# Layer 0 of a sequence model on one core: VectorE's token work with one PSUM operand, in halves inside the groups, and beta added to x ahead of time

## The chip, the cores and the metric

One kernel runs on one core of a Trainium2 chip. TensorE (PE) multiplies matrices and writes its results to PSUM; VectorE (DVE), ScalarE (ACT) and GpSimd (POOL) work elementwise; SyncE (SP) issues most of the DMAs. Each engine takes its own instructions in the order in which the program issues them, and waits for the others through semaphores. The metric is the device time of one execution in microseconds (us); lower is better.

## The reference, cut to what matters

```python
x = x + L0(_layernorm(x))        # a recurrence over 512 tokens, 8 sequences, width 128
x = x + FFN(_layernorm(x))       # six layers: local attention (16 heads, window 32) and a gated FFN

def L0(x):                       # x here is the normalised input
    xb = einsum('bsd,ed->sbe', x, B)
    h, y = tanh(h @ A.T + xb_t), h @ C.T          # token after token
    out = ys + x
    mu, var = mean(out), mean((out - mu) ** 2)
    return (out - mu) * rsqrt(var + 1e-5) * gamma + beta
```

So a token of the six layers is made in this way: y from the recurrence, plus the normalised input, a layernorm with gamma and beta ("the first norm"), plus x, and a second layernorm ("the second norm"). The first of those sums, x1, is also needed at the very end, and goes to DRAM. The tokens then enter the attention of the first layer of six; "layer 0" below is that first layer, which starts while the recurrence still runs.

## The kernel before, in words

**Chunks.** The 512 tokens are four chunks of 128; a chunk is a tile of 128 tokens on the partitions by 8 sequences by 128 features. `Recurrence.first(c)` loads x of a chunk (xc), normalises it (xn, pieces `a` and `b`), writes xn to DRAM, and turns it (piece `d`). It runs for chunk 0 at the start, and for chunks 1 to 3 between the first steps of the recurrence.

**Steps.** `step` is one token of the recurrence: a matmul of A with the last state into a PSUM bank that already holds B times the input (the tile xb), and a tanh on ScalarE. Inside the attention work a step is slipped in by `tick`, after each batch of matmuls. Where there is no other work, `alone` issues a step and two more matmuls that nobody reads (tile warm).

**Tokens of a chunk.** After the last step of a chunk, `queue(c)` makes a list of pieces: `output` (C times the states, in two halves of four sequences, tile yp, added to o), the first norm of o (`stats`, `rsqrt`, `normalise`), `scale` (times gamma, plus beta), `add` (x1 = x + o, to DRAM), the second norm of x1 into o, and `turn` for each half of the sequences (four transposes into PSUM, tile rt_c, and two ScalarE copies into xT, the token tile of the attention). All pieces between `output` and `turn` are VectorE's and work from SBUF to SBUF. `rsqrt` is eleven small instructions on 128 x 8 numbers.

**Groups.** The attention of layer 0 goes by groups: (chunk c, half h of the sequences, head group g), in the order of `parts`. A group is four slots, t = 0 to 3; each slot of `mixed` (used for the first nine groups, NREC) holds stages of several groups at once: scores (tile sc), max and exp, transposes (tp, at), the average (av), and for the group after next four "units" in slots 2 and 3. A unit is `unit_a` and `unit_b`: two matmuls (rawa, rawb), ScalarE squares, a VectorE product and two GpSimd operations of 128 x 1024. In slot 0 VectorE solves reciprocal roots (`Norms.solve`); in slot 1 these are spread by matmuls (tile bc) and multiplied in by `finish`, which also issues the DMAs to qT and kbuf; then four matmuls of `project` (tile yo). Later groups and layers use `dense`.

**What sets the order.** Program order, written out by hand: `run(k)` inside `mixed` puts the stages of `fill[k]` and then one waiting piece of the token work; in slot 1 only at k = 0, or pieces that need no PSUM bank. `begin(n)` calls `rec.need(c)` before the first group of a chunk: there all pieces that are left are issued at once, and if the recurrence has not got that far, steps alone.

**PSUM.** The pool "mm" has three banks while the recurrence runs. yp, rt_c, warm, raw, bc, yo and the others take turns in it.

Of the kernel before, what the change touches and what calls it, by code (L numbers as in the profile page):

```python
# [7 lines left out]
F32 = mybir.dt.float32  # L8
# [40 lines left out]
def mk_seq_preln_kernel(  # L49
# [28 lines left out]
    )  # L78
    x1_d = dram.tile([P, NT, B, D], F32, name="x1_d")
    xn_d = dram.tile([P, NT, B, D], F32, name="xn_d")  # L80
    xnT_d = dram.tile([P, NT, P, B], F32, name="xnT_d")
    kh_d = dram.tile([4, P, GP, NT, WINDOW], F32, name="kh_d")
    vh_d = dram.tile([4, 2, QB, NT, GP, VW], F32, name="vh_d")
# [68 lines left out]
    with tc.tile_pool(name="qk", bufs=2) as qkp, tc.tile_pool(  # L152
# [16 lines left out]
        class Recurrence:  # L169
# [17 lines left out]
                return x[:, c * P : (c + 1) * P, :].rearrange("b p d -> p b d")  # L187

            def stats(self, src, nm, bs=range(B)):
                if bs[0] == 0:  # L190
                    self.mv = small.tile([P, B, 2], F32, tag="mv", name=f"mv_{nm}", bufs=1)
                mv = self.mv
                for b in bs:
                    st = small.tile([P, 6], F32, tag="st", name=f"st_{nm}_{b}", bufs=4)
                    nc.vector.bn_stats(st, src[:, b, :])
                    nc.vector.bn_aggr(mv[:, b, :], st)

            def rsqrt(self, nm):
                x_, y, a = (
                    small.tile([P, B], F32, tag=f"r{i}", name=f"{i}_{nm}", bufs=1)  # L200
                    for i in "xya"
                )
                nc.vector.tensor_scalar_add(x_, self.mv[:, :, 1], EPS)
                nc.vector.tensor_scalar(
                    y.bitcast(I32), x_.bitcast(I32), -0.5, RSQRT_SEED, ALU.mult, ALU.add
                )
                for _ in range(3):
                    nc.vector.scalar_tensor_tensor(a, x_, -0.5, y, ALU.mult, ALU.mult)
                    nc.vector.tensor_mul(a, a, y)
                    nc.vector.scalar_tensor_tensor(y, a, 1.5, y, ALU.add, ALU.mult)  # L210
                self.rs = y

            def normalise(self, dst, src, bs=range(B)):
                for b in bs:
                    nc.vector.tensor_scalar(
                        dst[:, b, :],
                        src[:, b, :],
                        self.mv[:, b, 0:1],
                        self.rs[:, b : b + 1],
                        ALU.subtract,  # L220
                        ALU.mult,
                    )

            def turned(self, src, nm, q):

# [7 lines left out]
            def first(self, c):  # L233

                nm = f"a{c}"
                xc = self.load(c, self.x_of(c), "xc", "t", 4)
                xn = tmp.tile([P, B, D], F32, tag="sq", name=f"xn_{c}", bufs=4)
                if c:
                    xnT = tmp.tile([P, P, B], F32, tag="u", name=f"xnT_{c}")
                else:  # L240
                    xnT = self.xnT[0] = recp.tile([P, P, B], F32, tag="xnT", name="xnT_0")

                def a():
                    self.stats(xc, nm)

                def b():
                    self.rsqrt(nm)
                    self.normalise(xn, xc)
                    nc.sync.dma_start(xn_d[:, c], xn)

                def d():
                    for q in range(B // 4):
                        nc.vector.tensor_copy(
                            xnT[:, :, 4 * q : 4 * q + 4].rearrange("p t b -> p b t"),
                            self.turned(xn, nm, q),
                        )
                    if c:
                        nc.sync.dma_start(xnT_d[:, c], xnT)

                return [a, b, d]  # L260

            def step(self):
                t = self.t
# [25 lines left out]
                nc.scalar.activation(self.hT[:, tl, :], self.xb[:, k, :], AF.Tanh)  # L289
                self.t, self.work = t + 1, 0.0  # L290
                if tl == P - TB // 2:
                    self.o = self.load(c, xn_d[:, c], "o", "xf", 2)
                    self.x1 = self.load(c, self.x_of(c), "x1", "xf", 2)
                if tl == P - 1:
                    self.queue(c)
                    self.held = True
# [18 lines left out]
            def queue(self, c):  # L315
                o, x1 = self.o, self.x1

                def scale(bs):
                    g, b = (
                        gb[:, i : i + 1, :].to_broadcast([P, B // 2, D]) for i in range(2)  # L320
                    )
                    nc.vector.tensor_mul(o[:, bs, :], o[:, bs, :], g)
                    nc.vector.tensor_add(o[:, bs, :], o[:, bs, :], b)

                def add():
                    nc.vector.tensor_add(x1, x1, o)
                    nc.sync.dma_start(x1_d[:, c], x1)

                def turn(q):
                    tp = self.turned(o, f"c{c}", q)  # L330
                    sq = slice(4 * q, 4 * q + 4)
                    nc.scalar.copy(xT[:, sq, c * P : (c + 1) * P], tp)
                    nc.scalar.copy(self.edge[D // 2 :, sq, c], tp[D // 2 :, :, P - 1])
                    if q:
                        self.posted = c + 1

                def norm(dst, src, nm):
                    for b in range(0, B, 2):
                        yield lambda b=b: self.stats(src, nm, (b, b + 1)), False
                    yield lambda: self.rsqrt(nm), False  # L340
                    for b in range(0, B, 4):
                        yield lambda b=b: self.normalise(dst, src, range(b, b + 4)), False


                self.pieces = [(lambda q=q: self.output(c, o, q), True) for q in range(2)]
                self.pieces += norm(o, o, f"b{c}")
                self.pieces += [(lambda: scale(slice(0, 4)), False)]
                self.pieces += [(lambda: scale(slice(4, 8)), False), (add, False)]
                self.pieces += norm(o, x1, f"c{c}")
                self.pieces += [(lambda q=q: turn(q), True) for q in range(2)]  # L350

            def piece(self, bank=True):
                if self.pieces and (bank or not self.pieces[0][1]):
# [20 lines left out]
                if self.t < S and self.work >= PACE and not self.held and not late:  # L374
                    self.step()

            def need(self, c):

                while self.posted <= c:
                    if self.pieces:  # L380
                        self.piece()
                    else:
                        self.alone()

        rec = Recurrence()

# [551 lines left out]
        def begin(n):  # L938
# [3 lines left out]
            if l == 0:  # L942
                c, h = b
                if g == 0:
                    rec.need(c)
                    xs = shifted_chunk(c, h, buf)
                groups[n] = ChunkGroup(n, c, h, g, xs)
                return
# [10 lines left out]
        def mixed(n, t, cur, one, two, old, last, lt, back, bt):  # L959
# [21 lines left out]
            def run(k):  # L981
                for f in fill[k]:
                    f()
                if t != 1 or k == 0:
                    rec.piece()
                elif k < 4:
                    rec.piece(False)

            run(0)
            if cur:  # L990
# [3 lines left out]
            if back:  # L994
                back.turn_back(bt)
            run(1)
            if cur:
                cur.less_max(t)
            run(2)
# [5 lines left out]
                one.mask(0)  # L1005
            if one and t == 1:
                one.finish(1)
            if last:
                last.average(lt)
            if one and t == 1:  # L1010
                one.finish(2)
# [118 lines left out]
        with tc.manual_schedule():  # L1130
# [12 lines left out]
            while rec.t < P:  # L1143
                if rec.t % 8 == 7 and ahead:
                    ahead.pop(0)()
                rec.alone()
            for _ in range(2):
                rec.piece()
            while rec.posted == 0:
                rec.piece()  # L1150
                rec.alone()
            for t in (2, 3):
                slot(-2, t)
            feed = soon = None
            for n in range(-1, len(todo) + 1):
                m, l = n % GL, n // GL
                if n == NREC:
                    rec.need(NT - 1)
                    recs.close()
                    mmp = mms.enter_context(tc.tile_pool(name="mm", bufs=4, space=PSUM))  # L1160
                    ffn_w = load_ffn_weights(0)
# [142 lines left out]
```

## Time and profile before

| what | us |
|---|---|
| median of three runs | 3785.76 (3784.16 to 3793.64) |
| the profiled execution | 3782.38 |
| its span, first to last instruction | 3780.7 |
| PE busy, share of the span | 3549.9, 94% |
| VectorE busy | 2589.3, 68% |
| GpSimd busy | 1824.6, 48% |
| granted TensorE clock, mean of the span | 0.976 |

The recurrence takes place in the first 598 us of the span; what the change touches of the attention lies before 660 us. In the windows of the profile, the stretch from 0 to 650 us has granted clocks from 0.76 to 1.00, the stretch after it mostly 1.00. A busy share is read with care: PE's matmuls are pipelined and their ends are modelled, and an engine can be busy with an operation that itself is held up.

A group without token work lasts about 44 us while the recurrence runs: the scores matmuls of its four slots start at 291.68, 300.87, 316.51 and 324.47, and those of the next group at 335.81.

### The profile page before, as it was taken

The page shows a single profiled execution, that of the slowest core. Times are in us where ns is not written, and L with a number is a line of the kernel's source. Part 1 is how long each engine was busy: PE and PEld are TensorE (multiplying, and loading weights), DVE is VectorE, ACT ScalarE, POOL GpSimd, SP SyncE. Part 2 cuts the span into 40 slices and gives each one's busy share as a digit, 9 for nine tenths or more (in the row PEclk, how much of TensorE's full clock was granted, in tenths as well). Part 3 has the DMA queues.
Part 4 walks back from the last instruction along what each step waited for, and adds up shares of the span by engine and source line. Part 5 has one row for each costly group of instructions (what it writes and reads, how often), then busy time and mean ns, then how long its engine had stood idle before and what let it go on. Part 6 is the DMA issues. An engine that isn't in the chain of part 4 may idle for free.

```text
span 3780.7 us, 159055 instructions
## 1 busy us (share of the span) xinstructions
PE 3549.9 (94%) x70180; PEld 2140.3 (57%) x70180; DVE 2589.3 (68%) x5208; ACT 1932.6 (51%) x3864; POOL 1824.6 (48%) x780
## 2 busy tenths in 40 slices
PE   8889987999999999999999999999999999999997
PEld 4556665545556565556565555565565555555553
DVE  3455555767677677677677677677677677677673
ACT  2344443545555465455455455455455455455552
POOL 1333333625366366366366366365365355365450
PEclk9888988999999999999999999999999999999998
DMA  4233443554355355345356355355355355355342
GB/s 127 58 90 80 102 93 74 126 114 112 86 119 120 75 120 134 85 107 127 70 118 140 76 113 120 71 128 129 80 118 118 77 133 127 80 122 114 78 107 61
DMA packets 366074, 390.51 MB, mean 103 GB/s; under 512 B 96846, under 2 KB 262220, under 8 KB 365260
## 3 DMA queue, kind: packets, MB, share of 16 engines
q1 hardware_dynamic: 364380, 378.09, 43.8%
q8 instruction: 554, 9.08, 1.1%
q10 hardware_dynamic: 1008, 2.27, 0.2%
q14 instruction: 132, 1.08, 0.1%
HBM read 34.56 MB, written 14.20 MB: 13 GB/s over the span
## 4 chain that ended last, share of the span: by engine, by line
PE 75%; DVE 11%; SPq 4%; issue 4%; ACT 3%; DMA 3%; DVEq 0%; ACTq 0%
PE rawa L526 8%; PE rawb L538 8%; PE sc L627 7%; PE yo L713 5%; PE av L674 4%; PE nsq L430 4%; PE tp L656 4%; PE yf L912 3%; PE xb L281 3%; PE fa L886 3%; PE vps L587 3%; PE fg L890 3%; PE at L703 3%; SPq L574 3%; DMA xbuf<-xT 3%
## 5 line engine op out<-in xcount | busy, mean ns | idle before, releaser
L548 POOL TENSOR_TENSOR u<-rope_sb,bs 128x1024 f32<-128x1024 f32 x320 | 764.5, 2389 | 1263.1 <-ACT bs L544 901.5
L549 POOL TENSOR_TENSOR t<-t,u 128x1024 f32<-128x1024 f32 x320 | 757.3, 2367 | 25.1
L516 DVE SCALAR_TENSOR_TENSOR t<-rawa,par_sb,rope_sb 128x1024 f32<-128x1024 f32 x320 | 410.5, 1283 | 237.0 <-ACT sq L530 223.2
L565 DVE TENSOR_TENSOR t<-t,bc 128x1024 f32<-128x1024 f32 x320 | 381.8, 1213 | 13.6 <-PE bc L465 8.2
L650 ACT ACTIVATE e<-e 128x512 f32<-128x512 f32 x320 | 201.8, 630 | 354.4 <-DVE e L643 238.0
L526 PE MATMUL rawa<-xbuf,wqk 128*128 128x512 f32 x640 | 346.5, 623 | 30.5 <-DMA xbuf<-xT 30.3
L661 ACT COPY eT<-tp 128x512 f32<-128x512 f32 x320 | 190.2, 594 | 349.9 <-PE tp L656 349.2
L674 PEld LDWEIGHTS av<-vbuf,eT 64*32 64x32 f32 x20480 | 228.5, 105 | 218.7 <-issue 145.1
L538 PE MATMUL rawb<-xbuf,wqk 128*128 128x512 f32 x640 | 345.0, 621 | 0.0
L587 PE MATMUL vps<-wv,xbuf 128*64 128x256 f32 x2560 | 316.7, 386 | 7.8 <-DVE xf L864 6.6
L713 PE MATMUL yo<-aoT,wo 128*128 128x512 f32 x640 | 318.8, 621 | 0.9 <-ACT aoT L707 0.9
L627 PEld LDWEIGHTS sc<-kbuf,qT 64*32 64x32 f32 x20480 | 227.1, 105 | 146.5 <-issue 49.9
L674 PE MATMUL av<-vbuf,eT 64*32 64x65 f32 x20480 | 286.9, 225 | 6.7 <-issue 5.3
L640 DVE TENSOR_REDUCE mx<-sc 128x8 f32<-128x512 f32 x320 | 219.4, 686 | 103.7 <-PE sc L627 103.7
L692 DVE TENSOR_TENSOR ao<-av,rc 128x256 f32<-128x256 f32 x640 | 271.6, 424 | 22.0
L627 PE MATMUL sc<-kbuf,qT 64*32 64x64 f32 x20480 | 281.7, 225 | 3.8 <-issue 3.6
L281 PEld LDWEIGHTS xb<-hT,s1w 128*128 128x128 f32 x1022 | 170.3, 199 | 173.2 <-ACT hT L289 118.4
L542 ACT ACTIVATE sq<-rawb 128x512 f32<-128x512 f32 x320 | 189.9, 594 | 144.9 <-PE rawb L538 144.3
L587 PEld LDWEIGHTS vps<-wv,xbuf 128*64 128x64 f32 x2560 | 169.3, 136 | 150.8 <-DVE rc L691 35.6
L596 ACT COPY vbuf<-vps 128x512 f32<-128x512 f32 x320 | 188.3, 589 | 128.0 <-PE vps L587 124.1
L289 ACT ACTIVATE hT<-xb 128x8 f32<-128x8 f32 x512 | 91.8, 179 | 292.1 <-PE xb L281 278.1
L530 ACT ACTIVATE sq<-rawa 128x512 f32<-128x512 f32 x320 | 192.3, 601 | 80.8 <-PE rawa L526 80.7
(282 smaller groups left out, 6306.0 us busy)
## 6 DMA issues: line engine op xcount, KB each, us to landing
qT<-t SPq DMA_DIRECT2D x640, 128.0 KB
kbuf<-t SPq DMA_DIRECT2D x640, 128.0 KB
vbuf<-vbuf SPq DMA_DIRECT2D x544, 130.0 KB
vbuf<-vbuf SPq DMA_DIRECT2D x160, 97.5 KB
xbuf<-xT SPq DMA_DIRECT2D x95, 128.0 KB
xbuf<-xT SPq DMA_DIRECT2D x80, 127.8 KB
wqk<-in_w_qkv SPq DMA_DIRECT2D x12, 512.0 KB
xf<-xT SPq DMA_DIRECT2D x24, 256.0 KB
```

The source lines that it names most:

```text
L281: nc.tensor.matmul(self.xb[:, k, :], abc[:, 0, :], self.hT[:, (t - 1) % P, :], start=False, stop=True, skip_group_check=True,)
L516: nc.vector.scalar_tensor_tensor(t, self.twice(raw), scale, self.rope(isk, 1), ALU.mult, ALU.mult)
L526: nc.tensor.matmul(raw, self.wqk[:, c, 0], self.xs[:, WINDOW:], start=True, stop=True)
L538: nc.tensor.matmul(raw, self.wqk[:, c, 1], self.xs[:, WINDOW:], start=True, stop=True)
L548: nc.gpsimd.tensor_mul(self.wide(u), self.rope(isk, 0), self.twice(bs))
L549: nc.gpsimd.tensor_add(self.ts[c], self.ts[c], u)
L565: nc.vector.tensor_mul(t, t, self.bcs[c].unsqueeze(1).to_broadcast([P, 2, S]))
L587: nc.tensor.matmul(ps[par * KB : (par + 1) * KB, j], self.xs[:, k0 : k0 + KB], self.wv[:, par * GP * DH : (par + 1) * GP * DH], start=True ...
L627: nc.tensor.matmul(self.sc[blk * QB : (blk + 1) * QB, par, i, :], self.qT[rows, i, q0 : q0 + QB], kT[rows, i, :], start=False, stop=True, ...
L674: nc.tensor.matmul(av[blk * QB : (blk + 1) * QB, i, :VW], self.eT[rows, i, blk * QB : (blk + 1) * QB], self.v[rows, BT * t + blk, i, :], s ...
L692: nc.vector.tensor_mul(self.ao[t][:, :, par, :], av[:, :, :DH], rc.unsqueeze(2).to_broadcast([P, GP, DH]),)
L713: nc.tensor.matmul(self.yp, wo[:, self.g * GP + c, :], self.aoT[:, c, :], start=(c == 0), stop=(c == GP - 1),)
```

## The change

1. Pieces of a chunk now go by halves of four sequences: after both `output` pieces come, for each half, the statistics in two pieces, `middle` (root, first norm, gamma, sum with x, DMA of x1), statistics of x1 in two pieces, `last` (root, second norm), and `turn`. `need(c, h)` waits for one half only; the other is left for the slots of the groups that follow. In `need`, two steps alone follow each piece where the recurrence may go on.
2. `rsqrt` keeps its operands x_, a and the result r in a PSUM bank of the pool "mm"; only y is in SBUF. `normalise` becomes one instruction with r, spread over the row, as a tensor operand from PSUM. `affine` puts the first norm into the same bank, multiplies it by gamma there, and adds it to x1.
3. beta is added to x ahead of time: a piece `e` of `first(c)` adds it to xc in place and writes that to a new DRAM tensor xb_d, from which x1 is loaded.
4. In `mixed`, pieces may run in slots 2 and 3, in slot 0 and at k = 0 of slot 1 while the recurrence is held (that is, until `output` has run), and otherwise only those that need no bank; none else in slot 1.
5. In slot 1 of `mixed` the average stands before `less_max` and before the spread of the last unit.

```diff
     def rsqrt(self, nm, bs=slice(0, B)):
+        self.bank = mm(f"rs_{nm}")
+        x_, a, r = (self.bank[:, i * B : (i + 1) * B][:, bs] for i in range(3))
+        self.rs = small.tile([P, B], F32, tag="ry", name=f"y_{nm}", bufs=1)
+        y = self.rs[:, bs]
...
     def normalise(self, dst, src, bs=range(B)):
+        r = self.bank[:, 2 * B : 3 * B]
         for b in bs:
-            nc.vector.tensor_scalar(
+            nc.vector.scalar_tensor_tensor(
                 dst[:, b, :], src[:, b, :], self.mv[:, b, 0:1],
-                self.rs[:, b : b + 1],
+                r[:, b : b + 1].to_broadcast([P, D]),
                 ALU.subtract, ALU.mult,
             )
+    def affine(self, c, x1, o, bs):
+        r = small.tile([P, B], F32, tag="rz", name=f"rz_{c}_{bs.start}", bufs=1)
+        nc.vector.tensor_copy(r[:, bs], self.bank[:, 2 * B : 3 * B][:, bs])
+        z = self.bank.rearrange("p (b d) -> p b d", b=4)
+        for j in range(4):
+            b = bs.start + j
+            nc.vector.tensor_scalar(
+                z[:, j], o[:, b, :], self.mv[:, b, 0:1], r[:, b : b + 1],
+                ALU.subtract, ALU.mult,
+            )
+        nc.vector.tensor_mul(z, z, gb[:, :1, :].to_broadcast([P, 4, D]))
+        nc.vector.tensor_add(x1[:, bs], z, x1[:, bs])
+        nc.sync.dma_start(x1_d[:, c, bs], x1[:, bs])
...
+        def e():                                    # in first(c)
+            nc.vector.tensor_add(xc, xc, gb[:, 1:, :].to_broadcast([P, B, D]))
+            nc.sync.dma_start(xb_d[:, c], xc)
-        return [a, b, d]
+        return [a, b, d, e]
...
-            self.x1 = self.load(c, self.x_of(c), "x1", "xf", 2)
+            self.x1 = self.load(c, xb_d[:, c], "x1", "xf", 2)
...
+        def half(q):                                # in queue(c)
+            bs = slice(4 * q, 4 * q + 4)
+            rows = range(4 * q, 4 * q + 4)
+            def middle():
+                self.rsqrt(f"b{c}{q}", bs)
+                self.affine(c, x1, o, bs)
+            def last():
+                self.rsqrt(f"c{c}{q}", bs)
+                self.normalise(o, x1, rows)
+            for i in (0, 2):
+                yield lambda i=i: self.stats(o, f"b{c}", rows[i : i + 2]), False
+            yield middle, True
+            for i in (0, 2):
+                yield lambda i=i: self.stats(x1, f"c{c}", rows[i : i + 2]), False
+            yield last, True
+            yield lambda: turn(q), True
+        self.pieces += [(lambda q=q: self.output(c, o, q), True) for q in range(2)]
+        self.pieces += [*half(0), *half(1)]
...
-    def need(self, c):
-        while self.posted <= c:
-            if self.pieces:
-                self.piece()
-            else:
-                self.alone()
+    def need(self, c, h):
+        while self.posted <= 2 * c + h:
+            self.piece()
+            for _ in range(2):
+                late = self.t % P == P - TB // 2 and self.pieces
+                if self.t < S and not self.held and not late:
+                    self.alone()
...
     def run(k):                                     # in mixed
         for f in fill[k]:
             f()
-        if t != 1 or k == 0:
-            rec.piece()
-        elif k < 4:
-            rec.piece(False)
+        rec.piece(t >= 2 or rec.held and (t == 0 or k == 0))
...
     run(1)
+    if last and t == 1:
+        last.average(lt)
     if cur:
         cur.less_max(t)
...
-    if last:
+    if last and t != 1:
         last.average(lt)
...
-    for _ in range(2):
-        rec.piece()
-    while rec.posted == 0:
-        rec.piece()
-        rec.alone()
+    rec.need(0, 0)
     for t in (2, 3):
         slot(-2, t)
...
         if n == NREC:
-            rec.need(NT - 1)
+            rec.need(NT - 1, 1)
```

More of the change, by code (lines that the diff above doesn't have):

```diff
@@ L80, in mk_seq_preln_kernel @@
     xn_d = dram.tile([P, NT, B, D], F32, name="xn_d")
+    xb_d = dram.tile([P, NT, B, D], F32, name="xb_d")
     xnT_d = dram.tile([P, NT, P, B], F32, name="xnT_d")
@@ L189, in stats @@
             def stats(self, src, nm, bs=range(B)):
-                if bs[0] == 0:
+                if bs[0] % 4 == 0:
                     self.mv = small.tile([P, B, 2], F32, tag="mv", name=f"mv_{nm}", bufs=1)
@@ L196, in stats, with rsqrt @@
                     nc.vector.bn_aggr(mv[:, b, :], st)
[L198 to L203, printed above, removed]
+            def rsqrt(self, nm, bs=slice(0, B)):
+                self.bank = mm(f"rs_{nm}")
+                x_, a, r = (self.bank[:, i * B : (i + 1) * B][:, bs] for i in range(3))
+                self.rs = small.tile([P, B], F32, tag="ry", name=f"y_{nm}", bufs=1)
+                y = self.rs[:, bs]
+                nc.vector.tensor_scalar_add(x_, self.mv[:, bs, 1], EPS)
                 nc.vector.tensor_scalar(
@@ L206, in rsqrt @@
                 )
-                for _ in range(3):
+                for k in range(3):
                     nc.vector.scalar_tensor_tensor(a, x_, -0.5, y, ALU.mult, ALU.mult)
                     nc.vector.tensor_mul(a, a, y)
-                    nc.vector.scalar_tensor_tensor(y, a, 1.5, y, ALU.add, ALU.mult)
-                self.rs = y
+                    nc.vector.scalar_tensor_tensor(
+                        y if k < 2 else r, a, 1.5, y, ALU.add, ALU.mult
+                    )
             def normalise(self, dst, src, bs=range(B)):
+                r = self.bank[:, 2 * B : 3 * B]
                 for b in bs:
-                    nc.vector.tensor_scalar(
+                    nc.vector.scalar_tensor_tensor(
                         dst[:, b, :],
@@ L222, in normalise @@
                     )
+            def affine(self, c, x1, o, bs):
[5 more added lines that the diff above has]
+                    nc.vector.tensor_scalar(
+                        z[:, j],
+                        o[:, b, :],
+                        self.mv[:, b, 0:1],
+                        r[:, b : b + 1],
+                        ALU.subtract,
+                        ALU.mult,
+                    )
+                nc.vector.tensor_mul(z, z, gb[:, :1, :].to_broadcast([P, 4, D]))
+                nc.vector.tensor_add(x1[:, bs], z, x1[:, bs])
+                nc.sync.dma_start(x1_d[:, c, bs], x1[:, bs])
             def turned(self, src, nm, q):
@@ L249, in b @@
                     nc.sync.dma_start(xn_d[:, c], xn)
+                def e():
+                    nc.vector.tensor_add(
+                        xc, xc, gb[:, 1:, :].to_broadcast([P, B, D])
+                    )
+                    nc.sync.dma_start(xb_d[:, c], xc)
                 def d():
@@ L316, in queue @@
                 o, x1 = self.o, self.x1
[L318 to L327, printed above, removed]
                 def turn(q):
@@ L333, in turn @@
                     nc.scalar.copy(self.edge[D // 2 :, sq, c], tp[D // 2 :, :, P - 1])
[L334 to L350, printed above, removed]
+                    self.posted = 2 * c + q + 1
+                def half(q):
[16 more added lines that the diff above has]
+                self.pieces += [*half(0), *half(1)]
             def piece(self, bank=True):
@@ L944, in begin @@
                 if g == 0:
-                    rec.need(c)
+                    rec.need(c, h)
                     xs = shifted_chunk(c, h, buf)
```

## The prediction

> **What bounds the kernel now.** The page first: who is busy, and at what clock.
>
> ```profile
> PE 3549.9 (94%) x70180; PEld 2140.3 (57%) x70180; DVE 2589.3 (68%) x5208; ACT 1932.6 (51%) x3864; POOL 1824.6 (48%) x780
> PEclk9888988999999999999999999999999999999998
> ```
>
> PE is the bound, and its clock is below full only in the first slices, where the recurrence runs and the change lies. After 660 us PE has no gap that this change could touch, so whatever is won or lost before goes to the end one for one. Second view, the chain that ended last, cut to the ends of the chunks:
>
> ```profile
> 107.52 4.02 PE yp L302 x16
> ...
> 262.83 4.03 PE yp L302 x16
> 266.86 18.20 issue
> 285.06 2.22 PE rt_c L228 x8
> ...
> 601.74 18.20 issue
> ```
>
> Columns: start, length, what. After chunks 1 and 3 PE stands 18.20 us while VectorE goes through both norms of eight sequences. After chunk 0 the same time holds steps alone. Chunk 2 is made inside the groups; third view, a normal group's stretch and chunk 2's (window, its length, busy us of PE, PEld, VectorE, ScalarE and GpSimd, granted clock, DMA share, GB/s):
>
> ```profile
> 374.00:418.00 44.00, 42.78 (x773) 30.46 (x774) 24.65 (x50) 22.27 (x72) 18.68 (x9) 0.92 0.57 128
> 434.00:490.00 56.00, 39.22 (x547) 27.46 (x545) 44.67 (x107) 17.82 (x53) 20.62 (x8) 0.82 0.30 68
> ```
>
> PE does less in 56 us than in the 44 us, and VectorE is at 80%. From the scores of one group (425.02) to those of the next (495.64) it is 70.6 us, against 44.1 for a normal group (291.68 to 335.81): 26.5 over, of which 4.9 is the work of yp and of the next chunk's xb; 21.6 is token work in the way. Fourth view, the timeline of VectorE and of PE there:
>
> ```profile
> 471.34 2.72 DVE L323 TENSOR_TENSOR o<-o,s1w 128x512 f32<-128x512 f32 x1
> 475.31 2.07 DVE L326 TENSOR_TENSOR x<-x,o 128x1024 f32<-128x1024 f32 x1
> 485.62 2.19 DVE L208 SCALAR_TENSOR_TENSOR a_c<-x_c,y_c 128x8 f32<-128x8 f32 x1
> ```
> ```profile
> 489.85 2.27 PE L228 MATMUL rt_c<-ident,o 128*128 128x128 f32 x8 [5.04 <-DVE o L215]
> ```
>
> An operation of 0.17 us takes 2.19 while GpSimd works; such holds add up to some 8.7 us (L215 2.4, L322 1.05, L323 2.0, L326 0.6, L203 and L208 2.7, each over its length elsewhere). Then PE waits 5.04 us for the last of it.
>
> **The change part by part.**
>
> *Operands in PSUM.* Price: the same operation with one operand in PSUM (nsq) and with none:
>
> ```profile
> L455 DVE TENSOR_TENSOR a<-a,nsq 128x128 f32<-128x128 f32 x240 | 68.9, 287 | 8.3
> L455 DVE TENSOR_TENSOR a_f<-a_f,y_f 128x128 f32<-128x128 f32 x36 | 10.5, 292 | 1.2
> ```
>
> 287 against 292 ns: no cost, no gain, for the operation alone. [...] As to the holds: in the trace no operation with one PSUM operand (L750, L565, L643) is ever held, and none of the 96 statistics over 294 ns. So I take the holds as gone (worth up to 8.7 in chunk 2), the other end being that they stay.
>
> *A half's chain.* Chunk 1's rows give statistics 3.29 for eight (267.50 to 270.79), 1.65 for four; a root 2.21 (eleven instructions, to 273.00); a 128 x 128 normalise 0.257; a 512-wide product or sum 0.72; the copy 0.2. affine is 0.2 + 4 x 0.257 + 2 x 0.72 = 2.7; `middle` 4.9. From the last yp to the first transpose: 0.7 + 1.65 + 2.21 + 2.7 + 1.65 + 2.21 + 0.45 = 11.55 against 18.20: -6.65 at chunks 0, 1 and 3. At 1 and 3 four transposes leave as well, -1.1 each. So -6.65, -7.75, -7.75.
>
> *Steps alone.* Their number is 54 past the first 128 in both kernels, but two now follow each piece of `need`, so they lie under VectorE's chain: by the order of instructions 35 lay beside nothing before and 24 do after. 11 x 0.656 (a step alone at full clock): -7.2.
>
> *The second halves inside the groups.* This is what costs. In slot 2 `middle`, two statistics, `last` and `turn` are issued one after the other, and PE takes the transposes in order: behind them stand the third unit, the scores and the steps of the recurrence. Now the frame of a normal slot 2:
>
> ```profile
> 315.35 1.10 PE L526 MATMUL rawa_c1h<-xbuf,wqk 128*128 128x512 f32 x2
> ...
> 323.31 1.10 PE L526 MATMUL rawa_c1h<-xbuf,wqk 128*128 128x512 f32 x2
> ```
>
> The third unit starts 7.96 after the first. With chunk 1's second half VectorE has: the first unit's product until 3.3, `middle` 4.9, statistics 0.8, less_max 1.33, the second product 1.33, statistics 0.8, root 2.2, 0.3 of normalise = 15.0; the transposes take 1.0, third unit at 16.0: +8.1. After idle of 5 to 18 us the windows show PE at half clock for 4.1 to 4.6 us more, which loses 2.2: +10.3. Chunk 2's first half stands in the same frame (+10.3). Its second half has only `last` and `turn` there, before the second unit: 3.3 + 2.2 + 0.45 + 1.7 of normalises and transposes = 7.7 against 4.6, +3.1, and 1.6 of clock, +4.7. Chunk 2 thus pays 15.0 in place of 21.6: -6.6. Chunk 0's, before the fourth unit: 4.4 + two products 2.8 + 1.65 + 4.9 + 1.65 + 2.2 + 0.45 + transposes 1.1 = 19.1 against 8.94, +10.2, and clock 1.8: +12.0. Chunk 3's: 15.65 against 6.24, +9.4, clock 2.2, and two statistics before less_max, which slot 0's scores wait for, 1.65: +13.3. x1 goes to DRAM in two issues a chunk instead of one (0.34 each, as xn_d's below); SP waits there for `middle`, behind the issues of slot 1's `finish` and a group ahead of the next: 0, at most 0.34 a half. The bank that a half holds leaves two of three for the units; each is freed by a unit's product, which the chain above has in its place. The low bound of each half is 0: if VectorE were ahead in all, as a normal slot leaves it idle 1.2 to 3.8 us at a time.
>
> *e, and the order of DMAs.* In the opening the addition of beta (1.23 us for 1024 numbers) follows the turn of chunk 0 on VectorE, and the DMA to xb_d stands on SP ahead of the weights and of chunk 1's x:
>
> ```profile
> 15.29 0.34 SPq L249 DMA_DIRECT2D xn_d<-xn  x1
> 15.68 1.26 SPq L120 DMA_DIRECT2D wqk<-in_w_qkv  x2
> ...
> 18.70 6.79 SPq L183 DMA_DIRECT2D xc<-in_x  x3
> ```
>
> SP now waits for 17.16 + 1.23 = 18.4 where it went on at 15.68, so x of chunk 1 (landed 27.45) is 3.1 to 4.7 later. Its turn on PE had 0.55 slack: 2.5 to 4.1 of wait, 1.5 of clock: +4.5, bounds 0 (steps alone are fewer behind) and +6. The later chunks' `e` (1.23 each) lie under steps alone, VectorE being idle there; uncovered they cost 3.7.
>
> *Slot 1.* The average now stands ahead of the spread. Before, PE waits for the solve:
>
> ```profile
> 305.82 1.60 PE L465 MATMUL bc_c0h<-k_c0h,selt_sb 32*128 32x128 f32 x8 [1.05 <-DVE t_c0h L565]
> ```
>
> The average (0.86 for the same 64 matmuls at 321.09) stands in this gap. But the last spread (1.15 us) and its `finish` now come just ahead of `project`, whose wait is of the same size: 0, between -0.7 and +0.7 in nine slots. The clock falls to 0.50 for 6.2 to 6.7 us behind that gap (0.80 at 350.2, 0.50 to 357.4), about 3.1 us lost, nine times 28: won only if the new gap doesn't do the same. [...]
>
> **Sum.** +4.5 - 6.65 + 12.0 - 7.2 - 7.75 + 10.3 - 6.6 - 7.75 + 13.3 + 0 = +4.2. On the profiled execution, 3782.38, 3786.6; it lay 3.4 under the median, so 3790 against 3785.76.
>
> **The rivals.**
>
> B, slower: the holds stay. One fact for it: what holds L208 is GpSimd's 128 x 1024 work, and that work is in every slot 2, where the halves now are. Against it: no operand from PSUM was held. Price: 8.7 us a chunk, 4.4 a half, four halves on PE's way: +17.6, 3808. It decides from about 2 us a half, where the sum passes +11.4.
>
> C, faster: slot 1 loses its gap, and the clock stays up: -28 + 4.2, 3762. For it: 0.86 us of ready work stands where PE waited. Against: the last spread stays behind it, and its `finish` ahead of `project`.
>
> D, faster: the halves are hidden. If the second halves cost half of 10.3 + 10.3 + 4.7 + 12 + 13.3 = 50.6, the sum is -21: about 3768. For it: VectorE is idle a good third of a normal group. Against: one slot holds `middle`, `last` and `turn` without room between them.
>
> **How the numbers follow.** A measurement tells from no change about 0.3%, 11.4 us: 3774.4 to 3797.1. The forecast has 0.45, with a range of its own from 3776 to 3803 (opening 0 to 6, slot 1 ±6, each second half ±2.5); of it 0.04 lies under the band, 0.28 in it, 0.13 above. B has 0.27, above. C 0.15 and D 0.13, under. Faster 0.32, same 0.28, slower 0.40. The range of 3765 to 3812 leaves out about half of C, the low end of D and the high end of B, 0.2 in all.
>
> **What the profile after would show.** If right: the idle ahead of rt_c after chunks 1 and 3 is 11 to 12 us; in four slots 2 PE idles 5 to 8 us (1 to 2 for chunk 2's second half) ahead of four transposes, released by VectorE's o; x of chunk 1 lands near 31; no operation of the token work is over 1 us longer than its row here; the slots 1 keep a gap of about 1 us with a half clock behind it. B shows as 0.17-us operations that take 2; C as slot 1 at full clock; D as idle under 4 us ahead of the transposes. The prediction is wrong if the sum of these idles differs, or if a gap arises where none is named, above all in the opening or in dense layers after 660 us.

## The result, and the profile after

| | before | changed |
|---|---|---|
| median of 12 runs, us | 3784.72 | 3797.59 |
| lowest to highest, us | 3771.45 to 3795.83 | 3790.04 to 3811.74 |
| span of the profiled execution, us | 3780.7 | 3795.9 |

The ratio of the times is 1.0034, with a 95% interval of [1.0021, 1.0047]: the changed kernel is slower by 0.34%, some 13 us. The forecast was +4 us with a range of -21 to +26.

The page after, the same two lines as before: PE does 11 us more "busy" work with the same number of instructions, and the clock of the slices is about as it was.

```profile
PE 3560.9 (94%) x70180; PEld 2149.3 (57%) x70180; DVE 2603.9 (69%) x5304; ACT 1932.5 (51%) x3864; POOL 1824.8 (48%) x780
PEclk9898978999999999999999999999999999999998
```

The chain that ended last, at the ends of the chunks (start, length, what):

```profile
111.14 3.99 PE yp L332 x16
125.05 3.61 issue
128.66 1.22 PE rt_c L252 x4
...
275.96 4.00 PE yp L332 x16
289.81 3.64 issue
293.45 1.22 PE rt_c L252 x4
...
602.95 4.01 PE yp L332 x16
606.96 12.49 issue
```

After chunk 3 the 18.20 us of standing have become 12.49; after chunk 1 steps alone fill all but 3.64 of it. So the ends of the chunks did get shorter. The first yp, however, comes at 111.14 and not at 107.52.

Where the time went is read by pairing the same instruction in both traces: the start of each unit (tile rawa) and of yp, after minus before. The table gives how far that difference grows in each stretch; the last row leads to the spans' 15.2.

| stretch | forecast | measured |
|---|---|---|
| opening, to the first yp | +4.5 | +3.6 |
| end of chunk 0 | -6.65 | -4.6 |
| chunk 0's second half, in the groups | +12.0 | +13.2 |
| ends of chunks 1 and 3, with the steps alone | -22.7 | -3.5 and -14.9 |
| chunk 1's second half | +10.3 | +12.4 |
| slots 1 after it, and after chunk 2 | 0 | -3.4 and -3.6 |
| chunk 2 | -6.6 | +1.5 |
| chunk 3's second half | +13.3 | +11.6 |
| from there to 740 us, and to the end | 0 | +1.2 and +1.6 |

How a second half costs its 12 us is seen in chunk 1's. First what PE waits for from 320 to 345 us (who waits, for whom, us in total, times, longest), then the timelines of VectorE, ScalarE and PE there:

```profile
PE xb L311 <- ACT hT L319: 4.7, 1, 4.7
PE rt_c L252 <- DVE o L220: 2.8, 1, 2.8
```
```profile
332.34 0.69 DVE L245 TENSOR_TENSOR x<-rs_b,x 128x512 f32<-128x512 f32 x1
...
334.65 0.69 DVE L670 TENSOR_TENSOR e_c0h<-sc,mx_c0h 128x512 f32<-128x512 f32 x1
```
```profile
335.44 0.63 ACT L677 ACTIVATE e_c0h<-e_c0h 128x512 f32<-128x512 f32 x1 [4.76 <-DVE e_c0h L670]
...
336.49 0.17 ACT L319 ACTIVATE hT<-xb 128x8 f32<-128x8 f32 x1
```
```profile
336.71 0.60 PE L311 MATMUL xb<-hT,s1w 128*128 128x8 f32 x2 [4.71 <-ACT hT L319]
340.13 1.25 PE L252 MATMUL rt_c<-ident,o 128*128 128x128 f32 x4 [2.82 <-DVE o L220]
```

VectorE does `middle` (its last sum is L245) before the group's own difference from the maximum (L670). ScalarE's exponential waits 4.76 us for that, and as ScalarE takes its work in order, the tanh of the recurrence's step waits behind the exponential: the matmul that it needs ran on PE at 330.64, and it starts at 336.49. PE also goes in order and stands 4.71 us at the step, with the attention behind it. Only then does it reach the transposes, where 2.82 us are left to wait. Here the transposes are the smaller of two waits.

The first half of chunk 2 shows the same two waits (4.71 and 2.83). The second halves of chunks 0 and 3 show others; PE's longest in that of chunk 0 (134 to 160 us) and in that of chunk 3 (640 to 662 us):

```profile
PE rawb_c0h L565 <- DVE x L245: 4.2, 1, 4.2
PE rt_c L252 <- DVE o L220: 3.3, 1, 3.3
```
```profile
PE rt_c L252 <- DVE o L220: 9.4, 1, 9.4
```

At chunk 0 the larger wait is that of a unit's second matmuls (rawb): they don't read x, but they need the PSUM bank that `middle` gives back with its last sum, L245. At chunk 3 no step of the recurrence is left to stand at, and the whole wait is at the transposes. Each time PE waits for the same chain on VectorE; where it stands differs.

And chunk 2, where the forecast was off most. The timeline of PE, then granted clock by windows (window, length, busy us of PE, PEld, VectorE, ScalarE and GpSimd, clock, DMA share, GB/s) of the changed kernel, and of the kernel before over the same slots 0 and 1 of its own group:

```profile
506.00 1.09 PE L683 MATMUL tp_c1h<-ident,e_c1h 128*128 128x128 f32 x4 [1.46 <-DVE rc_c1h L718]
```
```profile
505.00:533.00 28.00, 27.00 (x298) 19.71 (x299) 14.92 (x39) 8.19 (x26) 1.50 (x1) 0.51 0.55 123
```
```profile
497.00:525.00 28.00, 26.78 (x397) 18.51 (x395) 14.75 (x29) 11.69 (x40) 0.00 (x0) 0.88 0.54 115
```

Behind a wait of 1.46 us (VectorE had the root and first norm of chunk 2's second half just ahead of the division) PE is granted 0.51 of its clock for 28 us, and gets through 298 recorded matmuls where it did 397. It is 27 us "busy" in both: a busy share doesn't show a halved clock.

### The profile page after: what moved, and what is told of

It is laid out like the page before. It is cut to its first block, busy times and chain, and to the rows that moved or that the text cites. A ratio compares the mean times of both kernels' runs of the same rounds, so it can differ in the third digit from the quotient of the medians.

```text
span 3795.9 us, 159183 instructions
## 1 busy us (share of the span) xinstructions
PE 3560.9 (94%) x70180; PEld 2149.3 (57%) x70180; DVE 2603.9 (69%) x5304; ACT 1932.5 (51%) x3864; POOL 1824.8 (48%) x780
## 4 chain that ended last, share of the span: by engine, by line
PE 75%; DVE 11%; SPq 4%; DMA 3%; ACT 3%; issue 3%; DVEq 0%; ACTq 0%
PE rawa L553 8%; PE rawb L565 8%; PE sc L654 7%; PE yo L740 5%; PE av L701 4%; PE nsq L457 4%; PE tp L683 4%; PE vps L614 3%; PE yf L939 3%; PE fa L913 3%; PE xb L311 3%; PE fg L917 3%; PE at L730 3%; SPq L601 3%; DMA xbuf<-xT 3%
## 5 line engine op out<-in xcount | busy, mean ns | idle before, releaser
L592 DVE TENSOR_TENSOR t<-t,bc 128x1024 f32<-128x1024 f32 x320 | 381.9, 1214 | 13.6 <-PE bc L492 8.2
```

The source lines that it names most:

```text
L592: nc.vector.tensor_mul(t, t, self.bcs[c].unsqueeze(1).to_broadcast([P, 2, S]))
```

## The experiments

Each kernel was timed against the kernel before on its own chip, on which the kernel before took 3760.8 to 3772.8 us; so ratios are compared, and starts of instructions up to 750 us. "Lost clock" below is the sum, over windows of half a us up to 760 us, of PE's busy time times what the clock lacked to full: 46.3 us before, 57.3 in the changed kernel.

**The changed kernel again.** No edit.

> The changed kernel, nothing altered, for a second trace. In the first one a wait of 1.46 us at 504.5 (transposes behind chunk 2's second half) was followed by 28 us of granted clock 0.50, 13.6 us of PE's work lost. If the wait brings the long stretch every time, it is there again and the span is within 4 us of 3796; if it was one execution's chance, the stretch is under 8 us long and the span about 9 us shorter.

Ratio 1.0025 [1.0015, 1.0035]. The stretch at half clock is there again, 28.0 us from 504.0, 13.7 lost (13.6 in the first trace). So it isn't one execution's chance, though it doesn't come every time either: of the runs below that keep this wait, the one with the average back has it (27.5 us), the one with e late has a shorter one, 14 us, that begins 10 us behind the wait. (These lengths are counted in windows of half a us. In the record of the clock in the traces of the kernel before and of the changed kernel, each of the 33 stretches at 0.50 that begin before 760 us lasts a whole multiple of 3.41 us; the long one of the first trace 8 x 3.41 = 27.3.) The opening differed: the first yp 1.4 us later than before, where the first trace had 3.6.

**e of chunk 0 after the weights.**

```diff
-            for f in ahead:
+            for f in ahead[:3]:
                 f()
...
-            ahead = [f for c in range(1, NT) for f in rec.first(c)]
+            ahead = ahead[3:] + [f for c in range(1, NT) for f in rec.first(c)]
```

> e of chunk 0 (beta added to x, its DMA) is issued after the weights and after chunk 1's load of x, between the first steps. If the opening's 3.6 us are SP's wait, x of chunk 1 lands near 27.5 (30.3 in the changed kernel, 27.45 before), the first yp starts at 107.5 to 108 in place of 111.1, and all later comes 3 to 4 us earlier. The rival, the addition itself on VectorE's path, leaves the first yp at 110 or later.

Ratio 1.0017 [1.0004, 1.0029]. The DMA queue of SyncE in the changed kernel, and here:

```profile
15.64 0.34 SPq L273 DMA_DIRECT2D xn_d<-xn  x1
18.59 0.32 SPq L279 DMA_DIRECT2D xb_d<-xc  x1
18.96 1.26 SPq L121 DMA_DIRECT2D wqk<-in_w_qkv  x2
...
21.96 6.28 SPq L184 DMA_DIRECT2D xc<-in_x  x3
```
```profile
16.39 1.26 SPq L121 DMA_DIRECT2D wqk<-in_w_qkv  x2
...
19.34 6.67 SPq L184 DMA_DIRECT2D xc<-in_x  x3
26.11 1.68 SPq L279 DMA_DIRECT2D xb_d<-xc  x1
```

The weights and chunk 1's x are issued 2.6 us earlier; the statistics of chunk 1 start at 27.97 and not at 30.32, and the first yp comes 0.4 us before that of the kernel before. The opening's cost is SyncE's wait, 1.8 to 4.0 us by the two traces of the changed kernel. The ratios alone don't tell the two kernels apart, and the span's 7 us hold the shorter stretch at half clock too.

**The average back in its place.**

```diff
-            if last and t == 1:
-                last.average(lt)
...
-            if last and t != 1:
+            if last:
                 last.average(lt)
```

> Only the average in slot 1 goes back to its old place. In the trace before a 1.05-us gap ahead of the last spread is followed by 7 to 7.5 us at half clock (3.4 us lost) in nine slots, in the changed kernel by 3.5 (1.7 lost) or none. If the move does that, undoing it brings the gaps and the long stretches back: +1.7 to +3 in each of nine, +15 to +25 in all. The forecast's own value, 0 with bounds of 6, would be within 6 us of the changed kernel.

Ratio 1.0037 [1.0024, 1.0050], span 3.8 us longer than that of the changed kernel on the same chip. PE's timeline in one slot 1, with the average put back, and in the changed kernel:

```profile
464.62 1.15 PE L492 MATMUL bc_c1h<-k_c1h,selt_sb 32*128 32x128 f32 x8 [1.05 <-DVE t_c1h L592]
465.70 0.86 PE L701 MATMUL av_c1h<-vbuf,eT_c1h 64*32 64x65 f32 x64
467.07 1.98 PE L740 MATMUL yo_c1h<-aoT_c1h,wo 128*128 128x512 f32 x2 [0.19 <-DVE t_c1h L592]
```
```profile
460.60 0.86 PE L701 MATMUL av_c1h<-vbuf,eT_c1h 64*32 64x65 f32 x64
461.72 1.15 PE L492 MATMUL bc_c1h<-k_c1h,selt_sb 32*128 32x128 f32 x8
464.18 1.45 PE L740 MATMUL yo_c1h<-aoT_c1h,wo 128*128 128x512 f32 x2 [1.30 <-DVE t_c1h L592]
```

The move changes a wait of 1.05 + 0.19 us for one of 1.30: the wait is not removed. Lost clock is 64.9 us here against 54.8 in the changed kernel there, yet by ratio and span only some 4 to 5 us are lost by the undoing, less than the 15 to 25 expected. That a faster PE gains nothing in stretches that wait for VectorE anyway is a likely reason; no run tries it.

**The average alone, in the kernel before.** The same edit the other way.

> The kernel before with only the average in slot 1 moved ahead. From the other side of the experiment that undid it (+3.8 us of span): gaps behind the spread go, and 7.5 us at half clock become 3.5 to 4 in most of nine slots: 1.5 to 2 us each at most, 3 to 15 in all, ratio 0.996 to 0.999. The forecast's value is 0 within 6 us.

Ratio 0.9985 [0.9971, 1.0000]. By the starts of the units it is 12.2 us ahead at 740 us, and lost clock is 30.0 us against 46.3. Before, eight slots 1 have a wait of 1.05 us and 6.8 us at half clock with it; of these, three now have 3.4 us, three none, and two still 6.8. So the part is worth having by itself, on the trace more plainly than by the times, whose interval reaches to no change.

**The transposes later.**

```diff
-                    yield lambda: turn(q), True
+                    yield lambda: turn(q), True, 2
...
+            def spread(self, bank, kinds):
+                if self.pieces and sum(self.pieces[0][2:]) in kinds:
+                    self.piece(bank)
...
-                rec.piece(t >= 2 or rec.held and (t == 0 or k == 0))
+                rec.spread(
+                    t >= 2 or rec.held and (t == 0 or k == 0),
+                    (0, 1) if t < 3 or k < 4 else (0, 2) if n > -2 else (0,),
+                )
```

> Only the transposes of a chunk's half, inside the groups, go from behind the norm to the end of slot 3 (chunk 0's: of the next group). VectorE's work stays where it is. If PE's wait for the end of that chain is the cost (the third units of the four second halves and of chunk 2's first are 13.2, 12.4, 11.6, 7.7 and 3.0 us later than before, 48 in all), most of it goes: 25 to 45 us less than the changed kernel, ratio 0.991 to 0.997 of before. The rival, that VectorE itself is late for the group (products, maxima, a PSUM bank held by the root), leaves PE waiting at other matmuls of those slots: less than 10 us gained.

Ratio 1.0032 [1.0019, 1.0044]: nothing gained that the times show; on the trace it is 5 us ahead of the changed kernel at 740 us. The first theory, which was also the prediction's, that the transposes are what PE's lost time hangs on, falls here. ScalarE's and PE's timelines of chunk 1's second half, with the transposes out of the way:

```profile
335.95 0.63 ACT L681 ACTIVATE e_c0h<-e_c0h 128x512 f32<-128x512 f32 x1 [4.75 <-DVE e_c0h L674]
```
```profile
337.21 0.60 PE L311 MATMUL xb<-hT,s1w 128*128 128x8 f32 x2 [4.70 <-ACT hT L319]
```

The wait ahead of the transposes is gone, the wait through the exponential and the tanh stands as it was. The half costs 9.0 us here (12.4 in the changed kernel). At chunk 3, where the transposes had the whole wait of 9.4 us, PE now stands 6.0 us at a unit, whose PSUM bank waits for a product of VectorE's: the wait finds another place.

**No token operand in PSUM.**

```diff
-                self.bank = mm(f"rs_{nm}")
+                self.bank = small.tile([P, 3 * B], F32, tag="rb", name=f"rs_{nm}", bufs=1)
...
-                z = self.bank.rearrange("p (b d) -> p b d", b=4)
+                z = o[:, bs]
```

> The changed kernel with x_, a, r and the first norm in SBUF: no token operand in PSUM. If the PSUM operand is what keeps GpSimd from holding VectorE, the holds of 1 to 2 us come back in the halves that lie in slots 2 and 3 (8.7 us for chunk 2 before), and the run is 5 to 20 us slower than the changed kernel (1.0025): ratio 1.004 to 1.008. If only GpSimd's idleness spared these operations, no operation of the token work is over twice its length elsewhere, and the time is within 3 us.

Ratio 1.0160 [1.0137, 1.0182], some 51 us over the changed kernel, beyond the range expected. VectorE's groups by form (busy us, mean ns of one, idle before) for one line of the root, in the changed kernel and here, and this run's timeline:

```profile
L210 DVE SCALAR_TENSOR_TENSOR rs_b<-rs_b,y_b 128x4 f32<-128x4 f32 x24 | 4.1, 170 | 0.8
```
```profile
L210 DVE SCALAR_TENSOR_TENSOR rs_b<-rs_b,y_b 128x4 f32<-128x4 f32 x24 | 12.0, 500 | 0.8
```
```profile
336.68 5.37 DVE L236 TENSOR_SCALAR o<-o,mv_b,rz 128x128 f32<-128x128 f32 x4
...
349.16 2.32 DVE L211 TENSOR_TENSOR rs_c<-rs_c,y_c 128x4 f32<-128x4 f32 x1
...
351.71 2.19 DVE L210 SCALAR_TENSOR_TENSOR rs_c<-rs_c,y_c 128x4 f32<-128x4 f32 x1
```
```profile
349.12 2.34 POOL L575 TENSOR_TENSOR u_c1h<-rope_sb,bs_c1h 128x1024 f32<-128x1024 f32 x1 [7.16 <-ACT bs_c1h L571]
351.54 2.34 POOL L576 TENSOR_TENSOR t_c1h<-t_c1h,u_c1h 128x1024 f32<-128x1024 f32 x1
```

Operations of 0.17 us take 2.2 to 2.3, about the length of the GpSimd operation that runs beside them (2.34), and end with it. Four normalises take 5.37; the same four take 1.11 in this run after chunk 3, where GpSimd is idle, and 1.76 in the changed kernel, which writes them to PSUM. In the changed kernel, in the same slots beside the same GpSimd work, none of the token work is held: of the 96 operations of lines 210 and 211 on a chunk's tokens, 31 overlap one of GpSimd's, and the longest takes 0.17 us. One operand in PSUM is what frees them, and in this arrangement it is the part of the change that pays.

**Both halves at the chunk's end.**

```diff
-                while self.posted <= 2 * c + h:
+                while self.posted <= 2 * c + 1:
```

> need waits for both halves of chunks 0, 1 and 3, so the second halves are made at the boundary, beside 14 steps alone at chunks 0 and 1, beside nothing at chunk 3; chunk 2 stays in the groups. The second halves in the groups cost 13.2, 12.4 and 11.6 us there; at the boundary a half takes 11.5 to 13.5, with some 9 us of steps alone under it that the groups no longer need. If those costs are the halves' own, the run comes out 5 to 20 us faster than the changed kernel, at 0.998 to 1.001 of before; if half a chain is hidden in the groups, it is slower than the changed kernel.

Ratio 1.0011 [0.9996, 1.0026], by the medians 5 us less than the changed kernel's ratio; the intervals overlap. By the starts of the units chunk 0's second half costs as much at the chunk's end as in the groups: at the eighth unit this run is 10.8 us behind the kernel before, and the changed kernel 12.3 and 11.1 in its two traces. From the last unit ahead of chunk 1's end to the fourth behind it this run loses 5.3 us and the changed kernel 10.0 and 8.2; over the same stretch at chunk 3 this one gains 10.0 and the changed kernel 3.3 and 5.1. So a second half, in the place where the change puts it, costs at least as much in the groups as outside.

**Pieces only where VectorE idles.** In the groups `middle` goes to the end of slot 0, `last` to the end of slot 1, the transposes to slot 2, statistics to the ends of slots (in the diff kind 0 is statistics, 1 `middle`, 2 `last`, 3 `turn`; `end` is the last of the nine groups).

```diff
-                rec.piece(t >= 2 or rec.held and (t == 0 or k == 0))
+                rec.spread(n, t, k)
...
+                        [(t, k) in ((0, 2), (0, 3)) or k == 4,
+                         (t, k) == (0, 4) or end and (t, k) == (1, 4),
+                         (t, k) == (1, 4) or end and (t, k) == (2, 4),
+                         t >= 2 and k == 3][kind]
```

> The pieces of a half go, inside the groups, to the places where VectorE idles (4.7 us at the end of slot 0, 3.8 at the end of slot 1): root, first norm and second statistics behind slot 0's last work, root and second norm behind slot 1's, the transposes in slot 2. Nothing else differs from the changed kernel. With late transposes alone PE still stood 5.2 us at a unit whose PSUM bank VectorE had not freed, and the run stayed as slow: if VectorE's place in the group is the cost, four halves lose about 8 us each less, 20 to 40 us in all, ratio 0.992 to 0.998 of before. If instead half the clock after any stop is what counts, or slot 0 and 1 have no such room, less than 8 us are gained.

Ratio 0.9966 [0.9952, 0.9980], 22 us less than the changed kernel by the two ratios. What PE waits for in chunk 1's second half (300 to 360 us):

```profile
PE bc_c0h L511 <- DVE x L245: 1.5, 1, 1.5
PE xb L311 <- ACT hT L319: 0.2, 1, 0.2
```

In the changed kernel PE's waits there are 9.0 us, 7.5 of them the two of above; here they are 1.7. From the last unit ahead of chunk 1's end to the fourth behind it, a stretch that holds the half in both kernels, this run loses 1.5 us (the changed kernel 10.0 and 8.2); at chunk 3 it gains 9.6 (3.3 and 5.1). That is no more than with both halves at the chunk's end (10.0): there PE now stands 4.4 us at slot 1's spread (tile bc), whose PSUM bank `middle` holds. Chunk 0's half, which comes where PE has little other work, still costs 12 (from 2.3 us ahead to 9.5 behind). That VectorE's place in the group was the cost of the halves of chunks 1 and 3 is shown.

It is not the whole gain. On the trace this run is 30 us ahead of the changed kernel at 740 us, and some 15 of the 30 arise in chunk 2, where the 28 us at half clock are 10 as well. How much of these 15 is waits and how much is clock, this run doesn't part.

**Bank pieces in slot 2 alone.**

```diff
-                rec.piece(t >= 2 or rec.held and (t == 0 or k == 0))
+                rec.piece(t == 2 or rec.held and (t != 1 or k == 0))
```

> The changed kernel, but token pieces that need a bank run in slot 2 alone once the recurrence is free (slot 3 no longer; yp as before). Chunk 2's second half so loses its root and first norm at the end of slot 3, behind which the transposes of the next slot 0 stood 1.46 us and the clock stayed at half for 28 us in both traces of the changed kernel. If that wait brought the 28 us, they are gone and the next group's first unit (519.43 before, 533.2 to 535.7 changed) comes 8 to 12 us earlier, against some 5 us more in slot 2 for that half: 2 to 8 us off the whole. If the clock falls for another reason, the stretch is still there.

Ratio 1.0018 [1.0008, 1.0028]. The same 28 us as above by windows, and PE's timeline in the next slot 2:

```profile
505.00:533.00 28.00, 26.53 (x445) 18.27 (x446) 14.26 (x35) 11.14 (x36) 1.05 (x1) 0.88 0.67 141
```
```profile
538.46 0.60 PE L311 MATMUL xb<-hT,s1w 128*128 128x8 f32 x2 [4.72 <-ACT hT L319]
541.88 1.25 PE L252 MATMUL rt_c<-ident,o 128*128 128x128 f32 x4 [2.82 <-DVE o L220]
```

Without the 1.46-us wait the clock is 0.88 in those 28 us, as it was before the change, and the next unit starts 5.6 us later than before, not 13.8 to 16.3. Then the half is made in slot 2 and costs 13.5 there, with the same two waits to a hundredth. What one place gives the other takes: no change that the ratio can tell.

**Spaced, and e late; then the tokens asked for one slot later.** The second adds to the first:

```diff
-                if t == 1 or n + 2 not in groups:
+                if t == 1 or n + 2 not in groups and (t or todo[n + 2][0]):
```

> The spaced pieces (0.9966 of before) with e of chunk 0 after the weights and chunk 1's load. If the two add up, 2 to 4 us less than spaced: ratio 0.9955 to 0.9962; if the opening's gain is taken back at the end of chunk 0, as the wait for VectorE there allows, 0.9966.

Ratio 0.9960 [0.9947, 0.9974].

> As spaced_e, and in layer 0 a chunk's tokens are asked for in slot 1 of the group in place of slot 0, so that slot 0's scores, transposes and values run ahead of the wait at the ends of chunks 1 and 3. If the slot gives VectorE a head start there, 5 to 10 us less than spaced_e, ratio 0.993 to 0.995; if the recurrence, which then ends later, or the load of the tokens takes it back, within 3 us of spaced_e.

Ratio 0.9955 [0.9942, 0.9969]: some 17 us faster than the kernel before. The first ratio lies where it was expected; the second is within 3 us of the first, the expectation's other case. Both intervals overlap that of the spaced pieces alone, so neither small part is shown by the times. On the trace the last is 22.8 us ahead of the kernel before at 740 us, spaced alone 16.5.

## Why the prediction was right, point by point

The forecast was slower by little, 3790 in 3765 to 3812; it was slower by 13, at the edge of what it called measurable. The sign came from the right place: the second halves in the groups cost more than the shorter ends of the chunks give.

- **The second halves, +12.0, +10.3, +13.3.** The sizes hold (13.2, 12.4, 11.6); the place was wrong for most of it. The prediction let PE idle "5 to 8 us" at the transposes in four slots 2. There it idles 3.3, 2.8, 2.8 and 9.4. The rest it stands elsewhere: 4.7 at a step of the recurrence, through the exponential and the tanh, in the slots of chunks 1 and 2, and 4.2 at a unit's PSUM bank in that of chunk 0, which the prediction took to be freed by the units' own products. The size came out because the same chain of VectorE's work was added up, and PE has to wait for its end in any case; but the prediction read the order of two engines where a third, ScalarE, stood between them. Moving the transposes, which the prediction's reading recommends, gains nothing that the times show; moving VectorE's work gains 22 us by the ratios, chunk 2's clock included.
- **Chunk 2, -6.6.** This is the term that failed: +1.5. It alone is 8 of the 11 us by which the sum fell short on the profiled executions (+4.2 against 15.2); the other misses largely cancel, which is luck. Its first half went much as said: 20.6 us from the second unit to the fourth, 8.0 in a normal slot, so 12.6 for 10.3; and `last` and `turn` of the second half cost 3.0 for 4.7. But the sum gave nothing for that half's `middle` at the end of slot 3. That piece makes a wait of 1.46 us, and the 28 us at half clock behind it lose 13.6 where the kernel before lost 3.4 in the same slots.
- **The ends of the chunks with the steps alone, -22.7.** -18.4, with some of the slot-1 gain in it. The chain summed to 11.55 takes 12.49 after chunk 3. Most of the difference is one price: four normalises take 1.76 us into PSUM and 1.11 into SBUF (the run without PSUM operands). The prediction's two rows, 287 and 292 ns, are of an operand read from PSUM, and it took them for a result written there as well. At chunk 0 -4.6 in place of -6.65.
- **The opening, +4.5.** Right in cause, as the late e shows; 1.4 and 3.6 in two traces. x of chunk 1 landed 2.9 us later.
- **Slot 1, 0.** The new wait is of the size of the old, as the forecast had it. But the clock behind it is back after 3.4 us, or doesn't fall, where it took 6.8, and that gave some 7 us. Rival C, which wanted 28, was right in a part of its mechanism.
- **Operands in PSUM.** That the holds would be gone was right, and rival B (holds in the groups) fell: no operation of the token work is held. The price for them being kept, +17.6, was too low: with SBUF operands it is some 51 us.
- **Rival D**, the halves hidden, didn't happen here; it is what the spaced pieces bring about in part, above all at chunk 1. The sign that was named for it, idle under 4 us ahead of the transposes, did appear in three of the four slots, with the halves at their full cost: a sign that watches one wait doesn't tell the two apart. Its time is mis-summed, too: 21 us under 3785.76 is 3765, not 3768.

## What to carry to other kernels

Before work is slipped into a slot, follow each engine's queue from the slipped-in piece on: what stands behind it on its own engine, which engine waits for that, and what is queued there in turn. At chunk 1 the chain VectorE, exponential, tanh, PE cost more (4.71 us) than the transposes that the eye goes to (2.82). And place a piece at the end of an engine's own work in the slot, where the profile shows the idle time, rather than where there happens to be a call.

## What the hardware showed that was not expected

- A short wait can be followed by a long stretch at half clock. 1.4 to 1.5 us without work were followed by 27.5 to 28 us at a granted 0.50 in three of four traces that have this wait, in slots 0 and 1; the waits of 4.7 and 2.8 us in slot 2 by 10 to 14 us, the waits among them. In the run without PSUM operands the wait at that place is 7.37 us, and within it begin 34 us at 0.50. Where a change of place took that wait away (late transposes, bank pieces in slot 2 alone, both halves at the chunk's end), no stretch from 500 to 560 us was longer than 14 us. What ends such a stretch was not tried by itself. Before the change, waits of 1.05 us come with 6.8 us at half clock in eight slots 1.
- The lengths at half clock were steps of 3.41 us: all 33 stretches at 0.50 that begin before 760 us in the traces of the kernel before and of the changed kernel are whole multiples of it. And equal waits came with different lengths: of the six waits of 1.30 us ahead of `project` in the changed kernel's trace up to 760 us, three have 3.41 us at half clock with them and three none.
- Whether GpSimd's work held VectorE's went here with where the operands lie: without PSUM operands, 0.17-us operations took 2.19 and 2.32 us beside GpSimd operations of 2.34; with one operand in PSUM, in the changed kernel, none of the 96 took more than its 0.17. A copy (2.26 us) and four normalises (5.37 us, 1.11 where GpSimd is idle) that read and wrote SBUF alone were held as well.
